# A graph network kernel: the factors of two heads in one mirrored block, and a new order of work

## The chip, the core and the metric

The kernel runs on one core of a Trainium2 chip. The core has five engines, each with its own queue, which it works off in order: TensorE (PE in the profile; its weight loads are shown as PEld) multiplies matrices, VectorE (DVE) and ScalarE (ACT) work element by element, GpSimd (POOL) does small side jobs, and SyncE (SP) issues the transfers between HBM and the on-chip memory SBUF. PE writes to PSUM, from which DVE and ACT read. Engines wait for each other by semaphores. The metric is the device time of one launch in microseconds.

## What is computed

For 16 graphs of 1024 nodes with 256 features: two layers, each with a residual and a layer norm. The first layer weighs the neighbours by a gate, the second is an attention with 4 heads of 64 columns. The change is in the second layer:

```python
Wh = (X @ W).reshape(B, N, H, F)
e_src = jnp.einsum('bnhf,hf->bnh', Wh, a_src)
e_dst = jnp.einsum('bjhf,hf->bjh', Wh, a_dst)
e = jax.nn.leaky_relu(e_src[:, :, None, :] + e_dst[:, None, :, :], LRELU_ALPHA)
mask = (A > 0)[..., None]
e = jnp.where(mask, e, NEG_INF)
alpha = jax.nn.softmax(e, axis=2)
Hout = jnp.einsum('bijh,bjhf->bihf', alpha, Wh)
Hout = jax.nn.elu(Hout)
```

## The kernel before

**The idea of the second layer.** The exponential of a leaky ReLU of a sum is a product of two factors, one of node i and one of node j, with one pair of factors where the sum is positive and another where it is negative. So per head there are two sets of columns of node j: `Wh` times the factor of the positive side (64 columns), `Wh` times that of the negative side (64), and the two factors themselves (2), E = 130 columns in all. A 0/1 matrix `pos` says for which edges the sum is positive. The sum over positive edges is a matmul of `pos` with the 130 columns; the negative side is the sum over all edges less the one over positive edges.

**Precision.** Each factor is held as a high and a low part (l = 0, 1), both in fp32r. They lie in one tile `gm`, by head, block of 128 nodes, part and column.

**Steps** (each is a generator; a step is one `yield`):
- First layer: `aload`, `cast`, `turn`, `mask` bring in and turn the adjacency; `xt`, `xta`, `score` (matmul `e`), `leak`, `leaky`, `sigmoid`, `below`, `lower`, `upper`, `self_loop` make the gate; `agg` multiplies gate and nodes; `residual` adds the bias and makes y; `moments0` (st), `gathered0` (mv), `spread0` (std and rstd, on POOL), `shift0` (DVE) and `norm0` (ACT) are the layer norm of y.
- Second layer: `yt`, `ytc` turn y; `project` is the matmul `pw`; `wh`, `sources`, `rows`, `keep_rows`, `top_dve`, `exps` make the factors, and `product`, `high`, `low` write them into `gm`.
- `pos` (L658): one DVE instruction makes 128 rows (nodes j) by 512 columns (half of the nodes i) for one head. There are 6 buffers.
- `acc` (L670): for each half and head, 8 blocks of j times 4 blocks of i, 32 matmuls of 260 columns: the high and low part of one head (2 x 130), read as one run. Four matmuls use one `pos`.
- `acc_low`, `acc_sum` (L693): ACT copies the low half out of PSUM, DVE adds it to the high half into `u`.
- `all_edges`, `total` (L713): the sums over all edges, without `pos`. Only the second 64 columns and the two factors are needed, 66 of each head: one matmul reads 4 runs of 66 columns for the 4 heads, 264 in all, 16 matmuls (8 blocks, 2 parts) for each block of i.
- `total_kept`, `total_less`, `weigh`, `divide`, `elu`, `join`: difference, weight, division and the elu, on `u`; then the second layer norm and the output.

**What sets the order.** Three tables, `FIRST`, `TIMES` and `LAST` (first graph, the 14 in the middle, last graph), give a place in time for each step of each generator, against the graph's own start; graphs start 112 units apart. `issue` sorts all steps of all graphs by their places and runs them, so that each engine gets its instructions in that order. The places are written out as numbers. No instruction passes another in an engine's queue.

Of the kernel before, what the change touches and what calls it, by code (L numbers as in the profile page):

```python
# [193 lines left out]
def stages(nc, k, pl, b, xg, adjg, outg, sums, span, zinv):  # L194
# [5 lines left out]
    HEADS = [(half, h) for half in range(NH) for h in range(H)]  # L200
# [3 lines left out]
    first, last, late = b == 0, b == k.B - 1, b >= k.B - 2  # L204
# [53 lines left out]
    def aload():  # L258
        for ib in range(NB):
            if first and 2 <= ib < 6:  # L260

                tile = pl.us.tile([P, 2, H, E], F32, tag="us", name="a_us")
                tile = tile.rearrange("p q h e -> p (q h e)")[:, 0:N].bitcast(I32)
            else:
                tile = pl.adjp.tile([P, N], I32, tag="a32", name="a32")
            t["a32", ib] = tile
            nc.sync.dma_start(out=t["a32", ib], in_=adjg[ib * P : (ib + 1) * P, :])
            yield
# [327 lines left out]
    def exps():  # L596
        es = t["es"] = small("es", 2, NB, H)
        nc.scalar.activation(es[:, 1], t["cm"], AF.Exp)
        nc.scalar.activation(es[:, 0], t["cm"], AF.Exp, scale=SLOPE)
        t["rho"] = small("rho", NB, H)  # L600
        nc.scalar.activation(t["rho"], t["sd"], AF.Exp, scale=SLOPE - 1.0)
        yield


    FACTORS = [(h, s) for h in range(H) for s in range(2)]
# [19 lines left out]
    def factor(h, s):  # L625
        if s == 0:
            yield slice(2 * F, E), t["es"][:, :, :, h].rearrange("p s b -> p b s")
        yield slice(s * F, (s + 1) * F), t["prod", h, s]

    def high():  # L630
        for h, s in FACTORS:
            for cols, val in factor(h, s):
                nc.scalar.copy(pl.gm[:, h, :, 0, cols], val)  # L633
            yield

    def low():
        for h, s in FACTORS:
            for cols, val in factor(h, s):
                hi = pl.gm[:, h, :, 0, cols].bitcast(F32)
                nc.vector.tensor_tensor(pl.gm[:, h, :, 1, cols], val, hi, ALU.subtract)  # L640
# [23 lines left out]
    def acc():  # L664
        for half, h in HEADS:
            for pair in range(NQ // 2):
                t["acc", half, h, pair] = pl.ps_u.tile([P, 2, HALF], F32, tag="u", name="acc")
            for jb in range(NB):
                for q in range(NQ):
                    nc.tensor.matmul(  # L670
                        t["acc", half, h, q // 2][:, q % 2, 0 : 2 * E],
                        lhsT=t["pos", half, h, jb][:, q * P : (q + 1) * P],
                        rhs=pl.gm[:, h, jb].rearrange("p l f -> p (l f)"),
# [14 lines left out]
    def acc_sum():  # L688
        for half, h in HEADS:
            for pair in range(NQ // 2):  # L690
                if h == 0:
                    t["u", half, pair] = pl.us.tile([P, 2, H, E], F32, tag="us", name="u")
                nc.vector.tensor_tensor(  # L693
                    t["u", half, pair][:, :, h, :],
                    t["acc", half, h, pair][:, :, 0:E],
                    t["low", half, h, pair], ALU.add,
                )
                yield

# [8 lines left out]
    def total():  # L708
        for ib in TOTALS:
            tot = t["tot", ib] = bank("tot")  # L710
            for jb in range(NB):
                for l in range(2):
                    nc.tensor.matmul(  # L713
                        tot[:, 0 : H * F1],
                        lhsT=t["allm", ib, jb // 4 * 4][:, jb % 4, :],
                        rhs=pl.gm[:, :, jb, l, F:E],
# [5 lines left out]

    def heads_of(tot):
        return tot[:, 0 : H * F1].rearrange("p (h f) -> p h f", h=H)
# [4 lines left out]

    def parts(half, pair, hs):  # L730

        u = t["u", half, pair][:, :, hs]
        return u[..., 0:F], u[..., F : 2 * F], u[..., 2 * F], u[..., 2 * F + 1]

    def second(half, pair):

        return t["u", half, pair][..., F : 2 * F + 1]
# [6 lines left out]
    def total_kept():  # L744
        for ib in TOTALS[:NQ]:
            pair, q = divmod(ib - NQ, 2)
            if q == 0:
                t["ts", pair] = pl.ts.tile([P, 2, H, F1], F32, tag="ts", name="ts")
            nc.scalar.copy(t["ts", pair][:, q], heads_of(t["tot", ib]))
            yield  # L750

    def total_less():
        for ib in TOTALS[NQ:]:
            u = second(0, ib // 2)[:, ib % 2]
            nc.vector.tensor_tensor(u, heads_of(t["tot", ib])[..., 0 : F + 1], u, ALU.subtract)
            yield

    PAIRS = [(half, pair) for half in range(NH) for pair in range(NQ // 2)]  # L760

    def times(val, by):

        if late:
            for q in range(2):
# [8 lines left out]
    def weigh():  # L774
        for half, pair in PAIRS:
            ib, hs = half * NQ + 2 * pair, heads(half)
            u2 = second(half, pair)[:, :, hs]
            if half:
                ts = t["ts", pair][:, :, hs, 0 : F + 1]
                nc.vector.tensor_tensor(u2, ts, u2, ALU.subtract)  # L780
                yield
            times(u2, t["rho"][:, ib : ib + 2, hs])
            yield

    def divide():
        t["rz"] = small("rzs", NB, H)
        for half, pair in PAIRS:
# [4 lines left out]
            rz = t["rz"][:, ib : ib + 2, hs]  # L792
# [8 lines left out]
    def join():  # L801
        for half, pair in PAIRS:
            o, ex, _, _ = parts(half, pair, heads(half))
            yp = nodes(half, pair)[:, :, heads(half)]
            rows = (0, 1) if last and half else (slice(0, 2),)
# [16 lines left out]
    def weigh_end():  # L822
        for h, pair in END:
            if last:
                u2 = second(1, pair)[:, :, h]
                nc.vector.tensor_tensor(u2, t["ts", pair][:, :, h, 0 : F + 1], u2, ALU.subtract)
# [43 lines left out]
    def leave():  # L870
# [32 lines left out]
    "xload": [-190.36],  # L903
    "aload": [-141.21, -134.94, -129.14, -126.41, -107.72, -95.92, -52.91, -49.35],
    "cast": [-133.33, -126.54, -110.85, -106.42, -72.33, -55.28, -40.89, -29.41],
    "turn": [-133.00, -118.97, -108.09, -86.35, -62.89, -45.14, -38.49, -26.07],
    "mask": [-126.25, -118.09, -94.06, -70.56, -52.12, -40.03, -32.69, -25.15],
    "setup": [-54.43, -50.76, -47.38],
    "xt": [-69.63, -66.83, -65.59, -61.38],
    "xtc": [-65.35, -64.69, -63.96, -57.76],  # L910
    "xta": [-60.02, -56.47, -53.23, -47.62, -40.80, -39.84, -35.73, -22.45],
    "score": [
        -55.95, -54.26, -52.86, -52.85, -50.30, -47.61, -41.77, -41.05, -37.61, -36.60,
        -31.53, -19.69,
    ],
    "leak": [
        -54.25, -52.28, -52.05, -51.99, -45.24, -41.19, -38.48, -36.59, -34.23, -28.07,
        -26.47, -19.19,
    ],
    "leaky": [  # L920
        -53.92, -51.61, -45.43, -45.41, -41.52, -40.38, -37.19, -36.20, -32.91, -26.88,
        -25.80, -17.05,
    ],
    "sigmoid": [-50.37, -36.56, -28.45, -23.28, -23.17, -15.81, -5.09, 4.38],
    "below": [-43.48, -40.73, -36.17, -28.75, -25.55, -24.80, -21.22, -11.11, 7.22, 7.95],
    "lower": [-41.97, -37.35, -33.23, -27.18, -24.41, -23.38, -19.01, -9.26, 8.37, 17.62],
    "upper": [-24.74, -21.21, -20.88, -18.06, 1.37, 12.57, 17.16, 22.61],
    "self_loop": [-22.52, -20.95, -18.10, -17.88, 3.26, 14.07, 18.13, 24.49],
    "agg": [
        -18.25, -16.27, -15.06, -15.02, -4.11, -4.03, -2.54, 0.32, 5.09, 8.13, 15.85,  # L930
        17.47, 21.46, 23.59, 23.78, 24.56,
    ],
    "residual": [-8.35, -7.46, -1.27, 2.37, 22.46, 22.48, 26.43, 27.74],
    "moments0": [-5.49, -4.53, 5.61, 8.01, 23.75, 25.11, 27.16, 28.13],
    "gathered0": [4.13, 6.42, 7.91, 10.51, 26.40, 27.32, 28.51, 29.05],
    "spread0": [13.40, 31.26],
    "shift0": [17.29, 31.54],
    "norm0": [21.66, 21.89, 22.47, 23.38, 34.53, 34.91, 35.50, 35.54],
    "yt": [27.46, 27.57, 36.68, 36.99],
    "ytc": [29.00, 29.33, 39.29, 39.57],  # L940
    "project": [32.52, 32.60, 33.90, 39.19, 40.28, 40.33, 40.41, 40.81],
    "wh": [33.22, 36.59, 37.58, 40.10, 40.68, 42.17, 42.34, 43.12],
    "sources": [41.16, 45.78],
    "rows": [41.83, 54.07],
    "keep_rows": [44.82, 56.53],
    "top_dve": [43.38, 45.01, 45.39, 50.81, 51.81],
    "top_pe": [44.42, 46.92],
    "exps": [51.81],
    "product": [53.02, 53.37, 53.98, 54.66, 58.34, 66.43, 69.20, 72.08],
    "high": [53.76, 54.40, 58.33, 58.56, 61.32, 68.49, 71.81, 73.63],  # L950
    "low": [54.19, 57.97, 61.74, 62.89, 71.04, 72.63, 75.29, 76.96],
    "sload": [50.80, 79.07, 83.92, 88.62, 102.34, 116.17, 128.36, 142.07],
    "pos": [
        57.31, 58.08, 60.13, 63.67, 69.85, 70.05, 71.57, 77.68, 80.69, 81.39, 82.09,
        82.79, 83.51, 84.84, 85.08, 85.50, 94.75, 97.25, 97.29, 97.48, 99.31, 100.22,
        100.86, 101.86, 104.39, 105.08, 105.66, 107.42, 108.55, 108.94, 109.06, 109.44,
        111.06, 112.18, 112.18, 112.50, 114.43, 114.99, 117.57, 118.23, 118.61, 122.99,
        125.51, 126.22, 128.00, 128.98, 130.58, 132.32, 133.80, 134.68, 135.40, 135.59,
        136.35, 141.70, 144.45, 144.66, 145.90, 146.60, 148.13, 149.39, 151.16, 153.05,
        156.93, 159.83,  # L960
    ],
    "acc": [
        66.06, 67.27, 68.14, 69.24, 71.32, 72.44, 73.71, 78.80, 83.16, 83.97, 84.72,
        85.39, 85.74, 87.50, 88.94, 90.52, 99.28, 99.52, 100.60, 101.24, 101.47, 101.85,
        102.15, 102.38, 108.43, 108.66, 109.45, 109.46, 109.72, 110.12, 110.70, 110.77,
        114.66, 115.11, 115.34, 116.25, 116.73, 118.20, 118.35, 119.33, 130.24, 130.46,
        130.54, 131.53, 132.09, 132.57, 134.85, 134.91, 141.46, 142.49, 142.93, 144.35,
        145.14, 145.81, 145.91, 146.87, 153.97, 154.83, 159.23, 159.59, 164.73, 165.20,
        165.32, 166.33,
    ],  # L970
    "acc_low": [
        79.49, 79.83, 96.76, 97.23, 103.47, 104.76, 112.24, 112.31, 122.02, 122.21,
        134.93, 135.59, 149.34, 149.98, 169.77, 170.85,
    ],
    "acc_sum": [
        80.66, 80.96, 97.10, 98.04, 105.15, 105.96, 112.53, 112.54, 127.47, 127.48,
# [501 lines left out]
```

## Time and profile before

| | |
|---|---|
| median of 3 runs | 1742.5 us (1742.15 to 1743.12) |
| span of the profiled execution | 1739.6 us |
| PE busy | 1692.1 us (97%) |
| DVE busy | 1639.6 us (94%) |
| ACT busy | 1239.4 us (71%) |
| POOL busy | 106.8 us (6%) |
| `acc` L670: matmuls, mean ns of one | 4096, 292 |
| `tot` L713: matmuls, mean ns of one | 2048, 297 |
| `agg` L427: matmul passes, mean ns of one | 2048, 379 |
| `pos` L658 on DVE: count, mean ns | 1024, 745 |
| u from `acc` and `low` L693 on DVE: count, mean ns | 256, 425 |

A line of the profile names the source line, the engine, the operation, what it writes and reads, the shape, the count, then the busy time in us, the mean duration of one in ns, and the idle time of the engine before it with what ended it. A matmul is pipelined: the next one starts before its duration is over, so its step, from start to start, is less than its duration. An fp32 matmul runs as two passes, and the profile counts passes; an fp32r matmul runs as one. The timeline gives start in us, duration in us and the instruction; equal neighbours are merged.

### The profile page before, as it was taken

What the parts mean: (1) busy time and instruction counts of PE and PEld (TensorE: products, weight loads), DVE (VectorE), ACT (ScalarE), POOL (GpSimd) and SP (SyncE); (2) the same over time, 40 slices, a digit from 0 to 9 for tenths busy, and PEclk for the clock granted to TensorE, in tenths of its full rate; (3) what the DMA queues carried; (4) which work ended last, traced back from release to release, by engine and by line L of the source; (5) the groups of instructions that cost most, each with busy time, mean ns of one, the idle gap of its engine ahead of it and who ended that gap; (6) DMA issues with size and microseconds to landing.
All of it is one profiled execution on the core that took longest, in us unless ns stands there. A gap on an engine that the chain in (4) does not pass through costs nothing.

```text
span 1739.6 us, 29647 instructions
## 1 busy us (share of the span) xinstructions
PE 1692.1 (97%) x10580; PEld 1492.5 (86%) x10580; DVE 1639.6 (94%) x3663; ACT 1239.4 (71%) x2766; POOL 106.8 (6%) x138
## 2 busy tenths in 40 slices
PE   8999999999999999999999999999999999999984
PEld 5789898998979889898998979889898898979883
DVE  5498999999999999999999999999999999999998
ACT  7674957759587685967759587685967859586784
POOL 0000000010000101000010000101000010000100
PEclk9999999999999999999999999999999999999987
DMA  5542333434334343333435334443343424422020
GB/s 190 129 116 67 98 98 92 110 92 131 88 89 101 105 125 92 94 101 92 109 92 129 91 86 102 105 128 91 89 107 92 110 67 117 105 71 55 26 68 26
DMA packets 249005, 168.59 MB, mean 97 GB/s; under 512 B 133010, under 2 KB 232468, under 8 KB 248852
## 3 DMA queue, kind: packets, MB, share of 16 engines
q1 hardware_dynamic: 248848, 166.63, 36.1%
q8 instruction: 86, 1.41, 0.3%
q14 instruction: 67, 0.55, 0.1%
q10 hardware_dynamic: 4, 0.00, 0.0%
HBM read 118.10 MB, written 17.04 MB: 78 GB/s over the span
## 4 chain that ended last, share of the span: by engine, by line
PE 91%; DVE 3%; ACT 2%; DMA 1%; issue 1%; POOL 0%; SPq 0%; ACTq 0%; DVEq 0%; POOLq 0%
PE acc L670 27%; PE agg L427 24%; PE tot L713 14%; PE e L356 13%; PE pw L517 7%; PE pg L395 3%; PE pt L498 2%; PE pt L319 1%; DVE pos L658 1%; DMA sbc<-sdram 1%; ACT prod L614 0%; DMA aT<-a 0%; PE pbc L591 0%; ACT gm L633 0%; ACT y L489 0%
## 5 line engine op out<-in xcount | busy, mean ns | idle before, releaser
L658 DVE SCALAR_TENSOR_TENSOR pos<-sbc,nd,mT 128x512 fp32r<-128x512 f32 x1024 | 737.4, 745 | 10.5 <-PE acc L670 5.0
L670 PE MATMUL acc<-gm,pos 128*128 128x260 f32 x4096 | 608.6, 292 | 8.9 <-DVE gm L640 5.0
L670 PEld LDWEIGHTS acc<-gm,pos 128*128 128x128 f32 x4096 | 536.8, 190 | 19.8 <-issue 5.7
L427 PE MATMUL agg<-xb,gate 128*128 128x256 f32 x2048 | 463.5, 379 | 0.2
L427 PEld LDWEIGHTS agg<-xb,gate 128*128 128x128 f32 x2048 | 379.9, 190 | 47.6 <-DVE gate L419 1.2
L713 PE MATMUL tot<-gm,allm 128*128 128x264 f32 x2048 | 328.8, 297 | 5.4 <-ACT gm L633 4.9
L713 PEld LDWEIGHTS tot<-gm,allm 128*128 128x128 f32 x2048 | 281.4, 189 | 9.7 <-ACT gm L633 5.1
L356 PE MATMUL e<-xT,xTa 128*128 128x512 f32 (+3 forms) x768 | 264.3, 489 | 2.2 <-ACT xTa L344 1.4
L356 PEld LDWEIGHTS e<-xT,xTa 128*128 128x128 f32 x768 | 135.1, 191 | 106.4 <-issue 55.3
L685 ACT COPY low<-acc 128x260 f32<-128x260 f32 x256 | 89.8, 377 | 187.5 <-PE acc L670 187.3
L705 ACT CAST allm<-mT 128x512 fp32r<-128x512 uint8 x256 | 157.4, 615 | 33.4 <-PE tot L713 31.7
L489 ACT ACTIVATE y<-y,shift,rstd 128x256 f32<-128x256 f32 x254 | 136.3, 592 | 48.6 <-DVE shift L477 48.6
L276 ACT ACTIVATE a<-a 128x1024 bf16<-128x1024 int32 x124 | 131.3, 1059 | 32.1 <-DMA aT<-a 23.0
L298 ACT ACTIVATE mT<-aT 128x1024 uint8<-128x1024 bf16 x120 | 127.1, 1059 | 7.6 <-DMA aT<-a 7.5
L468 POOL TENSOR_SCALAR std<-mv 128x4 f32<-128x4 f32 x64 | 27.7, 432 | 1618.7 <-DVE mv L450 1447.1
L517 PE MATMUL pw<-w_aug,yT 128*128 128x264 f32 x512 | 121.8, 387 | 0.5 <-ACT yT L507 0.5
L376 DVE TENSOR_TENSOR gate<-e,gate 128x512 f32<-128x512 f32 x192 | 105.5, 556 | 14.5 <-ACT gate L368 14.4
L693 DVE TENSOR_TENSOR u<-acc,low 128x260 f32<-128x260 f32 x256 | 103.1, 425 | 10.5 <-ACT low L685 10.3
L444 DVE BATCH_NORM_STATS2 st<-y 128x6 f32<-128x256 f32 x256 | 107.5, 421 | 1.2
L517 PEld LDWEIGHTS pw<-w_aug,yT 128*128 128x128 f32 x512 | 93.4, 190 | 15.4 <-ACT yT L507 1.9
L368 ACT ACTIVATE gate<-e 128x512 f32<-128x512 f32 x192 | 90.2, 486 | 13.7 <-PE e L356 13.3
L412 DVE TENSOR_TENSOR gate<-gate,mT 128x1024 f32<-128x1024 f32 (+7 forms) x128 | 96.6, 755 | 2.9 <-ACT mT L298 2.4
(111 smaller groups left out, 1788.8 us busy)
## 6 DMA issues: line engine op xcount, KB each, us to landing
a<-in_adj_dram SPq DMA_DIRECT2D x124, 512.0 KB, 4.6
sbc<-sdram SPq DMA_DIRECT2D x128, 256.0 KB, 4.6
out_dram<-y SPq DMA_DIRECT2D x31, 512.0 KB, 3.5
xb<-in_x_dram SPq DMA_DIRECT2D x15, 1024.0 KB, 5.4
a_us<-in_adj_dram SPq DMA_DIRECT2D x4, 512.0 KB, 8.9
aT<-a SPq DMA_TRANSPOSE x120, 3.1
xb<-in_x_dram SPq DMA_DIRECT2D x2, 512.0 KB, 4.7
sdram<-srow SPq DMA_DIRECT2D x32, 8.0 KB, 1.4
```

Of the source, the lines that this page charges most:

```text
L276: nc.scalar.activation(t["a16", ib], t["a32", ib], AF.Copy, accum_out=sums[:, 0, at : at + 1])
L298: nc.scalar.activation(t["mT"][:, :, ib * P : (ib + 1) * P], t["aT", ib], AF.Square, accum_out=sums[:, 1, at : at + 1],)
L356: nc.tensor.matmul(e[:, 0:n], lhsT=t["xTa", jb][:, c, :], rhs=t["xT"][:, c, at : at + n], start=(c == 0), stop=(c == DC - 1),)
L376: nc.vector.tensor_tensor(ge, t["e", jb, at][:, 0:n], ge, ALU.max)
L427: nc.tensor.matmul(agg[:, 0:D], lhsT=t["gate"][:, jb, ib * P : (ib + 1) * P], rhs=t["xb"][:, jb, :], start=(jb == 0), stop=(jb == NB - 1),)
L444: nc.vector.bn_stats(st, t["y", half][:, q, :])
L489: nc.scalar.activation(y, y, AF.Identity, bias=shift, scale=rstd)
L517: nc.tensor.matmul(pw[:, 0:WD], lhsT=t["yT"][:, c, jb * P : (jb + 1) * P], rhs=k.w_aug[:, c, :], start=(c == 0), stop=(c == DC - 1),)
L658: nc.vector.scalar_tensor_tensor(p_, t["sbc", half, h], t["nd"][:, jb, h : h + 1], t["mT"][:, jb, half * HALF : (half + 1) * HALF], ALU.is ...
L670: nc.tensor.matmul(t["acc", half, h, q // 2][:, q % 2, 0 : 2 * E], lhsT=t["pos", half, h, jb][:, q * P : (q + 1) * P], rhs=pl.gm[:, h, jb] ...
L705: nc.scalar.copy(m_, t["mT"][:, j0 : j0 + 4, ib * P : (ib + 1) * P])
L713: nc.tensor.matmul(tot[:, 0 : H * F1], lhsT=t["allm", ib, jb // 4 * 4][:, jb % 4, :], rhs=pl.gm[:, :, jb, l, F:E], start=(jb == 0 and l == 0),
```

## The change

**The layout.** Two heads share a block of 260 columns for each block of nodes and part. The even head's columns stand as before (positive side 64, negative side 64, factor of the negative side, factor of the positive side), the odd head's mirrored (the two factors, negative side, positive side). The second parts of both, 66 columns each, then lie side by side: 132 columns in one run. So `total` reads two runs of 132 in place of four of 66; `acc` reads one head's columns as two runs of 130 (high and low part), in place of one run of 260. The last graph keeps the old layout.

**What follows from it.** `exps` makes the three factors in a row (slope, one, slope), one Exp more in 15 graphs, so that both kinds of head can copy their pair. `acc_sum` writes a head's 130 columns as two overlapping pieces of 66 (264 elements instead of 260) into `u`, which has 132 columns a head now; the piece of the odd head spoils two columns, which the even head's write puts right. So the heads go in the order 1, 0, 3, 2, in `product`, `high`, `low`, `sload`, `pos`, `acc` and all that follows. Views of `u`, `tot` and `ts` are made anew for `weigh`, `divide`, `join`.

**The tables.** All three tables of places are new. A few lines of each kind are shown.

```diff
+    ORDER = [*range(H)] if last else [h ^ 1 for h in range(H)]
+    HEADS = [(half, h) for half in range(NH) for h in ORDER]
...
-        es = t["es"] = small("es", 2, NB, H)
+        es = t["es"] = small("es", 3, NB, H)
         nc.scalar.activation(es[:, 1], t["cm"], AF.Exp)
-        nc.scalar.activation(es[:, 0], t["cm"], AF.Exp, scale=SLOPE)
+        for s in (0, 2)[: 1 if last else 2]:
+            nc.scalar.activation(es[:, s], t["cm"], AF.Exp, scale=SLOPE)
...
+    AT = [(0, F, 2 * F), (0, F, 2 * F) if last else (F + 2, 2, 0)] * (H // 2)
+
+    def gm_of(h):
+        if last:
+            return pl.gm.rearrange("p (h b l e) -> p h b l e", h=H, l=2, e=E)[:, h]
+        pairs = pl.gm.rearrange("p (g b l i e) -> p g i b l e", g=H // 2, l=2, i=2, e=E)
+        return pairs[:, h // 2, h % 2]
+
+    def gm_second(jb, l):
...
+        pairs = pl.gm.rearrange("p (g b l e) -> p g b l e", g=H // 2, l=2, e=2 * E)
+        return pairs[:, :, jb, l, F : F + 2 * F1]
...
-                        rhs=pl.gm[:, h, jb].rearrange("p l f -> p (l f)"),
+                        rhs=gm_of(h)[:, jb],
...
-                nc.vector.tensor_tensor(
-                    t["u", half, pair][:, :, h, :],
-                    t["acc", half, h, pair][:, :, 0:E],
-                    t["low", half, h, pair], ALU.add,
-                )
+                    at = h // 2 * 2 * (E + 2)
+                    at, step = (at + E + F1, -F1) if h % 2 else (at, F1)
+                    nc.vector.tensor_tensor(
+                        view(t["u", half, pair][:, :], at, [H * (E + 2), 2], [step, 2], [1, F1]),
+                        view(acc[:, :, :], 0, [HALF, 2], [F, 2], [1, F1]),
+                        view(low[:, :, :], 0, [E, 2], [F, 2], [1, F1]), ALU.add,
+                    )
...
-                        tot[:, 0 : H * F1],
+                        by_pair(tot[:, 0 : H * F1]),
...
-                        rhs=pl.gm[:, :, jb, l, F:E],
+                        rhs=gm_second(jb, l),
...
-    "spread0": [13.40, 31.26],
-    "shift0": [17.29, 31.54],
+    "spread0": [19.80, 33.29],
+    "shift0": [20.95, 33.72],
```

**The order that comes out** around the second half of the first layer norm, in a graph of the middle, as the instructions stand in PE's and DVE's queue (`xN`: N in a row; fp32 matmuls counted once, not by passes):

```
before  PE:  agg x12 | pt<-y x8 | acc x16 | pw x4 | acc x8 | pw x2 | acc x8 | pt<-y x8 | pw x10
before  DVE: y | st | mv x2 | pos | y<-u (L810) | u<-u,y (L807) | shift | pos x2 | y<-u | pos | st | pos
after   PE:  acc x12 | pt<-y x4 | agg x8 | pw x6 | acc x28 | pt<-y x4 | acc x4 | pt<-y x4 | pw x4
after   DVE: y | st | mv | pos x2 | shift | pos x2 | u<-u,y (L881) | pos x3 | mv | y<-u (L884) | st | pos
```

PE enters `acc` or `tot` from another kind of matmul 387 times in the order before, 417 times in the new one. ACT loads its function tables 87 times before, 37 times after. All other counts of instructions are the same.

## The prediction

> **What bounds the kernel now.** I read the page's first part, the busy time of the engines over two middle periods, the chain of waits, a stretch of the timeline, and the waits of PE near the end, in this order.
>
> ```profile
> span 1739.6 us, 29647 instructions
> ...
> PE 1692.1 (97%) x10580; PEld 1492.5 (86%) x10580; DVE 1639.6 (94%) x3663; ACT 1239.4 (71%) x2766; POOL 106.8 (6%) x138
> ```
>
> ```profile
> core 0: us, PE busy (x) PEld busy (x) DVE busy (x) ACT busy (x) POOL busy (x), PEclk, DMA share, GB/s
> 847.70:952.20 104.50, 104.50 (x660) 92.70 (x659) 102.34 (x227) 76.05 (x167) 6.60 (x8) 1.00 0.39 102
> 952.20:1056.60 104.40, 104.40 (x658) 92.60 (x658) 102.28 (x227) 75.95 (x166) 6.59 (x8) 1.00 0.38 102
> ```
>
> Each window is one graph's period (from one graph's first `agg` matmul to the next's). PE is busy in all of its 104.4 us, at full clock; DVE in 102.3, so 2.1 us a period are left to it; ACT has 28 idle. So PE sets the period, with no gap left to remove, and DVE stands 2% behind it: any piece of work that DVE delivers late makes a PE gap that nothing gives back. The rest of the span, 1739.6 less 16 periods, is the first graph's start and the end.
>
> The chain of waits gives PE's real step (the mean duration of a matmul overlaps its neighbours):
>
> ```profile
> 888.81 2.87 PE acc L670 x24
> ...
> 894.36 5.18 PE agg L427 x24
> ...
> 907.80 4.45 PE pw L517 x20
> ...
> 937.40 1.50 PE tot L713 x12
> ```
>
> Per matmul: `acc` 119.6 ns for 260 columns in one run, `tot` 125.0 ns for 264 columns in four runs of 66, `agg` 215.8, `pw` 222.5. At `acc`'s rate per column 264 columns would take 121.4, so the four runs cost 3.6 ns more.
>
> **The change on PE: lengths of runs.** It touches 15 of the 16 graphs (the last keeps the old form): 15 x 128 = 1920 `tot` matmuls go from four runs to two, and 15 x 256 = 3840 `acc` matmuls from one run to two. With 3.6 ns spread over three breaks, a break costs 1.2 ns: `tot` gains 1920 x 2.4 = 4.6 us, `acc` loses 3840 x 1.2 = 4.6 us. **Sum 0.** Bounds: `tot` gains all 3.6 and `acc` pays nothing, -6.9 us; `tot` gains half of it (1.8) and `acc` pays 1.8, as an odd head's runs begin at another offset than an even one's, -3.5 + 6.9 = +3.4 us. I take 0, since `acc` in two runs lies between two rows that I have, one run and four.
>
> The Trainium skill ("SBUF — State Buffer", in its note on SBUF cachelines) has lines of 16 bytes and a price for each new line. By it a `tot` of four 264-byte runs touches 68 lines and of two 528-byte runs 66; an `acc` goes from 65 to 66. The row that bears on this is the 3.6 ns. Scaling each row by its lines, an estimate from that page, `tot` would lose 125.0 x 2/68 = 3.7 ns and `acc` gain 119.6/65 = 1.8: -7.1 + 7.1 us, again nothing. The rule speaks against the change, as the cheap side is hit twice as often.
>
> **DVE, ACT, SP.** `acc_sum` adds 264 instead of 260 elements (240 times). From 416 ns for 256 (L459, y) and 691 for 512 (L790, u): 1.07 ns an element, so 4.3 ns x 240 = 1.0 us on DVE, 0.07 a period, hidden in its 2.1 idle; if the interleaved write cost more, 50 ns a call would be 0.8 us a period, which still fits, though it makes every late delivery later. The other operations on `u` keep their counts and sizes (65- and 64-column runs, three free dimensions). ACT gets one Exp of 32 elements in 15 graphs (row L599, 213 ns): 3.2 us, in ACT's idle. In the new order ACT loads its tables 37 times instead of 87: 50 x 1.283 us (row L382) = 64 us of ACT, which wasn't on the path either. SP's queue has the same transfers, at other places. The order of heads 1, 0, 3, 2 costs nothing itself: the two columns that the odd head's sum leaves wrong are written by the even head's, later on the same engine.
>
> **The new order is the term that decides.** Before, in the steady state, the chain holds PE alone; the longest runs of `acc` on PE are 24. In the new order each of 14 graphs has 28 `acc` in a row, at the worst place: last `agg`, 6 `pw`, 28 `acc`. On DVE stand, after that `agg`: y, st, mv, two `pos`, `shift`, two `pos`, one addition to u (L881), three `pos`. `shift` waits for POOL, and behind it are the `pos` that the 28 need (four matmuls use one `pos`). The same sequence, as it runs now:
>
> ```profile
> 1005.45 0.39 DVE L459 TENSOR_TENSOR y<-agg,bias_bc 128x256 f32<-128x256 f32 x1
> 1005.87 0.43 DVE L444 BATCH_NORM_STATS2 st<-y 128x6 f32<-128x256 f32 x1
> ...
> 1006.60 0.63 POOL L468 TENSOR_SCALAR std<-mv 128x4 f32<-128x4 f32 x1 [17.25 <-DVE mv L450]
> ...
> 1007.32 1.33 POOL L469 TENSOR_TENSOR rstd<-std,mhalf 128x4 f32<-128x4 f32 x1
> ...
> 1008.68 0.16 DVE L477 SCALAR_TENSOR_TENSOR shift<-mv,rstd 128x4 f32<-128x4 f32 x1 [0.32 <-POOL rstd L469]
> 1008.76 1.41 DVE L658 SCALAR_TENSOR_TENSOR pos<-sbc,nd,mT 128x512 fp32r<-128x512 f32 x2
> ```
>
> ```profile
> 969.24 2.74 DVE L658 SCALAR_TENSOR_TENSOR pos<-sbc,nd,mT 128x512 fp32r<-128x512 f32 x4
> 971.89 0.43 DVE L459 TENSOR_TENSOR y<-agg,bias_bc 128x256 f32<-128x256 f32 x1
> ```
>
> From y to the `pos` behind `shift` are 3.31 us, whatever DVE does meanwhile, since POOL sets it; a `pos` then takes 0.66 from start to start, 0.75 to its end; the addition to u 0.60 (1002.90 to 1003.50 in this stretch). So, from y's start: the first `pos` begins at 3.31, the second at 3.97, the addition at 4.63, the third `pos` at 5.23, and it ends at 5.98. y itself starts 0.2 us later than PE's next matmul (an `agg` lasts 0.379 by its row and steps by 0.216; 0.04 for the release): 6.18. On PE 6 `pw` (two passes each) take 12 x 0.2225 = 2.67 and 24 `acc` 2.87: the 25th is due at 5.54. The third `pos` behind `shift` is the seventh of this run, the one that the 25th needs. Late by 0.64 us. Now, with `pos` two places ahead of the need and 8 or 16 `acc` at a time between the `pw`, the same wait of `shift` (0.32) reaches no PE gap. What hides it there is that PE has `pw` and transposes between the short runs.
>
> I take 0.6 us x 14 = **+8.4 us**. Bounds: 0, if an older `pos` stands ready, and 0.84 x 14 = +11.8, the whole time that `shift` waits in this order (3.23 less y, st, mv and two `pos`, 0.42 + 0.34 + 0.30 + 1.33 = 2.39). What is late next is the transpose of y's second half and with it the projections, which have only ACT's idle before them, no further loss.
>
> Entering `acc` or `tot` from another kind of matmul happens 417 times in the new order instead of 387. In the chain, four `acc` that follow other work take 0.47 to 0.48 us, where 4 x 0.1196 is 0.478; an entry can't cost over 20 ns. I take +0.2 (0 to 0.6).
>
> The last 160 us have their own table, and there PE does wait (us in total, times, longest):
>
> ```profile
> PE pm L1424 <- DVE bad L1422: 15.3, 1, 15.3
> PE acc L670 <- DVE gm L640: 5.0, 1, 5.0
> PE tot L713 <- ACT gm L633: 4.9, 1, 4.9
> PE acc L670 <- DVE u L693: 3.8, 3, 2.6
> ```
>
> The first is the final check's wait for the output's last steps. Of the other 13.7 us a new order may save or add a few. What can be priced: 44 `acc` of the last graph stand ahead of its first `tot`, where 32 stood, and such a run goes at DVE's pace, 0.66 us for a `pos` against 0.48 for its four `acc`: three more `pos` are +0.5. The last 64 `acc` stand alone in both orders. I take +0.5, bounds -3 and +4. The first graph's start, with some 11 us of PE waits, I leave at 0 (-2 to +2).
>
> **Sum** 0 + 8.4 + 0.2 + 0.5 = +9.1 against the span of 1739.6, so 1748.7. The median of the runs is 2.9 above this execution's span (1742.5); the change doesn't touch what lies around it: **1752**.
>
> **Rivals.** (1) *Faster: the runs of 132 pay and the order holds.* `tot` gains 3.6 ns, `acc` pays nothing, and the late `pos` is there in time, because DVE gets ahead by its 2.1 us a period: 1742.5 - 6.9 + 0.7 = 1736. For it: 130 contiguous columns are long against 66. Against: the chain after `agg` goes through POOL, so spare time on DVE doesn't shorten it. It decides where the gap is under 0.25 us a graph. (2) *No change:* the same gain, the gap as computed: 1742.5 - 6.9 + 8.4 + 0.7 = 1745. (3) *Worse:* `acc` pays as in the upper bound (+3.4), the gap is 0.84 (+11.8), and the end adds 3: 1761. For it: DVE has only 2% left, so that one late transfer or sum pushes several `pos`; against: nothing that DVE does becomes longer by more than 5 ns. That the change doesn't do what it says I leave out: `tot` is built with two runs, and the number of matmuls is the same.
>
> **Numbers.** The forecast has 0.57, its own range 1746 to 1758; rival 1 0.17, rival 2 0.11, rival 3 0.15. 0.2% is 3.5 us, about what can be told from no change: faster (below 1739) 0.17, the same 0.11, slower 0.72. The range goes from 1739, which leaves out most of rival 1, to 1762, above rival 3.
>
> **What would show it.** In the profile after: `tot` at about 122.5 ns a step and `acc` at about 121, in the chain; a gap of 0.6 us on PE in each middle graph, at an `acc` that waits for DVE's `pos` while DVE's `shift` waited about 0.8 for POOL; periods of 105.0 instead of 104.4. If the periods are 104 or less and PE is busy throughout, the step with the late `pos` was wrong. If `acc` stays at 119.6 the price of a break was. If the middle periods are as computed and the time is not, the end was.

## The result, and the profile after

| | before | after |
|---|---|---|
| median (5 runs each) | 1742.5 us (1742.15 to 1744.48) | 1773.35 us (1771.33 to 1776.62) |
| span of the profiled execution | 1739.6 us | 1769.5 us |
| start to the first `agg` | 35.9 us | 35.4 us |
| first period | 76.8 us | 76.8 us |
| the 14 middle periods | 1466.8 us | 1495.8 us |
| from the last graph's first `agg` to the end | 160.2 us | 161.6 us |

The change makes the kernel slower, by a ratio of 1.0174 [1.0163, 1.0185]. The forecast was +9.5 us, the result is +30.9, and 29.0 of the span's 29.9 lie in the 14 middle periods: 2.07 us in each, where 0.6 was forecast.

The page's first part and two groups of its fifth, after:

```profile
span 1769.5 us, 29462 instructions
...
PE 1702.6 (96%) x10580; PEld 1492.8 (84%) x10580; DVE 1647.1 (93%) x3663; ACT 1176.8 (67%) x2731; POOL 110.6 (6%) x138
...
L692 PE MATMUL acc<-gm,pos 128*128 128x260 f32 x4096 | 626.2, 299 | 30.3 <-DVE pos L680 17.5
...
L754 PE MATMUL tot<-gm,allm 128*128 128x264 f32 x2048 | 309.8, 294 | 0.5 <-ACT allm L746 0.5
```

`acc` (L692, before L670) has become longer, 292 to 299 ns, `tot` (L754, before L713) shorter, 297 to 294. Both are small. The new entry is the 30.3 us of idle time ahead of `acc`, most of it waits for `pos`. Two middle periods show the same as a share of the period (columns as before: length, then busy time of each engine):

```profile
859.10:965.60 106.50, 105.20 (x660) 92.70 (x659) 102.19 (x226) 70.61 (x163) 7.07 (x8) 1.00 0.39 100
965.60:1073.30 107.70, 105.76 (x660) 92.57 (x659) 103.53 (x228) 71.42 (x163) 7.07 (x8) 1.00 0.38 99
```

PE was busy in all 104.4 us of a period before; now 1.3 to 1.9 us of each are empty. The clock is 1.00 as before, and ACT has about five us less work per period than before.

**Where the gaps lie.** Counted from PE's starts (a step over 0.08 us longer than the usual one of its form), the gaps of the 14 middle graphs sum to 33.0 us, 4.4 before. By their place after the graph's first `agg`: about 24 us, 13.7 in sum (11 graphs with 0.9 to 1.2 each, and a step 0.1 too long behind it); about 61 us, 11.2 (13 graphs: 0.67, with 0.1 just ahead of it and 0.1 behind it); 16 to 18 us, 1.7. The other 6.4 are 2.0 more than all gaps before; 2.8 of them are 28 steps around `pbc`, 0.1 too long each, which the kernel before has as well. The one at 61 us is the gap of the forecast. The timeline of after there:

```profile
914.57 0.63 POOL L471 TENSOR_SCALAR std<-mv 128x4 f32<-128x4 f32 x1 [18.62 <-DVE mv L453]
...
915.29 1.39 POOL L472 TENSOR_TENSOR rstd<-std,mhalf 128x4 f32<-128x4 f32 x1
...
916.71 0.16 DVE L480 SCALAR_TENSOR_TENSOR shift<-mv,rstd 128x4 f32<-128x4 f32 x1 [0.93 <-POOL rstd L472]
916.79 1.41 DVE L680 SCALAR_TENSOR_TENSOR pos<-sbc,nd,mT 128x512 fp32r<-128x512 f32 x2
...
918.12 0.69 DVE L881 SCALAR_TENSOR_TENSOR u<-u,y 128x512 f32<-128x512 f32 x1
...
918.72 2.07 DVE L680 SCALAR_TENSOR_TENSOR pos<-sbc,nd,mT 128x512 fp32r<-128x512 f32 x3
919.52 0.76 PE L692 MATMUL acc<-gm,pos 128*128 128x260 f32 x4 [0.52 <-DVE pos L680]
```

`shift` waits 0.93 us for POOL, two `pos`, the addition and one more `pos` follow, and PE's `acc` at 919.52 waits for that third `pos`. (The idle time of 0.52 goes by modelled ends; from start to start the step is 0.67 too long.)

The gap at 24 us was in no step of the prediction. The chain of waits of after, which before held PE alone there, shows how it comes about (start, duration, what):

```profile
1293.04 1.05 ACT mT L301 x2
1294.11 3.99 DMA aT<-a
1298.20 1.15 ACT a L279 x2
1299.36 1.28 ACT L890
1300.65 0.64 ACT u L890
1301.29 1.03 ACT mT L301 x2
1302.62 0.77 DVE u L727 x2
1303.39 0.61 DVE u L881
1304.03 0.69 DVE y L884
1304.92 0.66 DVE pos L680
```

It starts in the adjacency of a later graph. `mask` (L301) reads a turned piece; the next transposing DMA (`turn`) may then be issued and takes 3.99 us; `cast` (L279) needs its end, since the bf16 tile that it writes is the one that the DMA reads. Behind `cast` in ACT's queue stand a table load, an exp, the next `mask` and two `acc_low`; DVE's `u` (L727) waits for those, and behind `u` stand the `pos` that PE needs. The timeline of an earlier graph has the amounts, in square brackets:

```profile
763.79 1.06 ACT L279 ACTIVATE a<-a 128x1024 bf16<-128x1024 int32 x1 [4.38 <-DMA aT<-a]
...
768.20 0.77 DVE L727 TENSOR_TENSOR u<-acc,low 128x264 f32<-128x264 f32 x2 [1.97 <-ACT low L709]
...
776.19 0.76 PE L692 MATMUL acc<-gm,pos 128*128 128x260 f32 x4 [1.04 <-DVE pos L680]
```

ACT stands still for 4.38 us, DVE for 1.97 of them, PE for 1.04: each engine swallows a part with the work that it has ahead. The new table has `cast[2]` at -120.51 and `turn[1]`, whose end it needs, at -120.58, 0.07 units ahead. In the old one they stand 8.1 apart (-110.85 and -118.97). The waits of after by pair (us in total, times, longest):

```profile
ACT a L279 <- DMA aT<-a: 63.1, 18, 4.6
...
DVE u L727 <- ACT low L709: 23.4, 15, 2.5
...
DVE shift L480 <- POOL rstd L472: 19.7, 20, 1.5
...
PE acc L692 <- DVE pos L680: 17.5, 25, 1.0
```

The same four before:

```profile
ACT a L276 <- DMA aT<-a: 23.0, 16, 2.8
...
DVE u L693 <- ACT low L685: 10.3, 14, 1.3
...
DVE shift L477 <- POOL rstd L469: 9.0, 17, 1.5
...
PE acc L670 <- DVE pos L658: 0.2, 1, 0.2
```

### The profile page after: what moved, and what is told of

Its sections match the earlier page's. It is cut to its first block, busy times and chain, and to the rows that moved or that the text cites. A ratio compares the mean times of both kernels' runs of the same rounds, so it can differ in the third digit from the quotient of the medians.

```text
span 1769.5 us, 29462 instructions
## 1 busy us (share of the span) xinstructions
PE 1702.6 (96%) x10580; PEld 1492.8 (84%) x10580; DVE 1647.1 (93%) x3663; ACT 1176.8 (67%) x2731; POOL 110.6 (6%) x138
## 5 line engine op out<-in xcount | busy, mean ns | idle before, releaser
L680 DVE SCALAR_TENSOR_TENSOR pos<-sbc,nd,mT 128x512 fp32r<-128x512 f32 x1024 | 723.6, 744 | 1.4 <-PE acc L692 1.0
L692 PE MATMUL acc<-gm,pos 128*128 128x260 f32 x4096 | 626.2, 299 | 30.3 <-DVE pos L680 17.5
L692 PEld LDWEIGHTS acc<-gm,pos 128*128 128x128 f32 x4096 | 541.3, 190 | 68.9 <-DVE pos L680 23.6
L430 PE MATMUL agg<-xb,gate 128*128 128x256 f32 x2048 | 468.6, 380 | 1.2 <-DVE gate L422 1.2
L754 PE MATMUL tot<-gm,allm 128*128 128x264 f32 x2048 | 309.8, 294 | 0.5 <-ACT allm L746 0.5
L754 PEld LDWEIGHTS tot<-gm,allm 128*128 128x128 f32 x2048 | 271.1, 189 | 4.6 <-ACT allm L746 0.8
L709 ACT COPY low<-acc 128x260 f32<-128x260 f32 x256 | 84.4, 372 | 202.4 <-PE acc L692 200.8
L359 PEld LDWEIGHTS e<-xT,xTa 128*128 128x128 f32 x768 | 130.7, 191 | 85.8 <-issue 47.4
L279 ACT ACTIVATE a<-a 128x1024 bf16<-128x1024 int32 x124 | 131.4, 1059 | 66.9 <-DMA aT<-a 63.1
L301 ACT ACTIVATE mT<-aT 128x1024 uint8<-128x1024 bf16 x120 | 126.9, 1058 | 7.1 <-DMA aT<-a 7.1
L520 PE MATMUL pw<-w_aug,yT 128*128 128x264 f32 x512 | 122.1, 388 | 0.4 <-ACT yT L510 0.4
L727 DVE TENSOR_TENSOR u<-acc,low 128x264 f32<-128x264 f32 x240 | 96.1, 426 | 24.4 <-ACT low L709 23.4
L447 DVE BATCH_NORM_STATS2 st<-y 128x6 f32<-128x256 f32 x256 | 103.7, 415 | 1.3
```

The costliest lines, as they stand in the source:

```text
L279: nc.scalar.activation(t["a16", ib], t["a32", ib], AF.Copy, accum_out=sums[:, 0, at : at + 1])
L301: nc.scalar.activation(t["mT"][:, :, ib * P : (ib + 1) * P], t["aT", ib], AF.Square, accum_out=sums[:, 1, at : at + 1],)
L359: nc.tensor.matmul(e[:, 0:n], lhsT=t["xTa", jb][:, c, :], rhs=t["xT"][:, c, at : at + n], start=(c == 0), stop=(c == DC - 1),)
L430: nc.tensor.matmul(agg[:, 0:D], lhsT=t["gate"][:, jb, ib * P : (ib + 1) * P], rhs=t["xb"][:, jb, :], start=(jb == 0), stop=(jb == NB - 1),)
L447: nc.vector.bn_stats(st, t["y", half][:, q, :])
L520: nc.tensor.matmul(pw[:, 0:WD], lhsT=t["yT"][:, c, jb * P : (jb + 1) * P], rhs=k.w_aug[:, c, :], start=(c == 0), stop=(c == DC - 1),)
```

## The experiments

All times are medians in three rounds beside the kernel before on the same chip, 1743.19 us for the first four and 1742.9 for the other four.

**1 and 2: layout and order apart.** The first has the new layout and order of heads with the three old tables of places, the second the old layout with the new ones.

```diff
 TIMES = {
...
-    "cast": [-130.00, -124.39, -120.51, -103.41, -71.16, -47.91, -42.40, -29.83],
-    "turn": [-128.78, -120.58, -113.47, -87.75, -58.61, -46.85, -35.79, -23.68],
+    "cast": [-133.33, -126.54, -110.85, -106.42, -72.33, -55.28, -40.89, -29.41],
+    "turn": [-133.00, -118.97, -108.09, -86.35, -62.89, -45.14, -38.49, -26.07],
...
```

> The changed kernel with the three tables of the kernel before. Theory A (the order costs the time): only the steps of the matmuls differ, 3840 acc at +1.9 ns (119.6 to 121.5 in the two traces) and 1920 tot at -2.6 ns (125.0 to 122.4), so +7.3 - 5.0 = +2.3 us: 1745 us, periods near 104.5 us, no PE gap over 0.2 us in a middle graph. Theory B (the layout makes DVE or PE late, the order only shows it): most of the 31 us stay, 1765 us or more.

> The kernel before with the three new tables; heads in order 0, 1, 2, 3, the old factors. Theory A: the gaps of the new order are there without the layout: 1773 less 2.3 is 1771 us, with PE gaps of about 1.2 us (near 24 us after a graph's first agg) and 0.7 us (near 61 us) in each middle graph. Theory B: 1745 us, no such gaps.

The new layout in the old order takes 1745.85 us, ratio 1.0015 [1.0005, 1.0024]; the old layout in the new order 1772.78, 1.017 [1.0153, 1.0187]. So the order costs the time, and the layout costs 0.15%. In the first neither gap is there, and its middle periods take 2.1 us more than before, about what the lengths of its matmuls make. In the second both gaps are there (1.05 us at 23.6, 0.68 at 60.5), with `tot` and `acc` at their old lengths. Equal pieces of the chain of waits, first before, then the first experiment:

```profile
366.32 2.87 PE acc L670 x24
...
416.90 2.58 PE tot L713 x20
```

```profile
365.81 2.92 PE acc L692 x24
...
416.57 2.53 PE tot L754 x20
```

24 `acc` have become 0.05 us longer, 20 `tot` 0.05 shorter. Over the 15 graphs that have the new layout the mean step of `acc` goes from 119.8 ns to 121.7, that of `tot` from 125.3 to 122.6: 3840 x 1.9 = 7.3 us lost and 1920 x 2.65 = 5.1 gained, +2.2.

**3, 4 and 5: each gap by itself.** The third moves a `cast` and the `mask` of the new table to later places, so that other ACT work comes ahead of the wait; the fifth moves only the second `shift`, behind two more `pos`; the fourth does both.

```diff
-    "cast": [-130.00, -124.39, -120.51, -103.41, -71.16, -47.91, -42.40, -29.83],
+    "cast": [-130.00, -124.39, -117.10, -103.41, -71.16, -47.91, -42.40, -29.83],
-    "mask": [-121.17, -118.70, -101.41, -79.33, -54.12, -37.09, -29.23, -20.61],
+    "mask": [-121.17, -117.00, -101.41, -79.33, -54.12, -37.09, -29.23, -20.61],
```

```diff
-    "shift0": [20.95, 33.72],
+    "shift0": [20.95, 34.58],
```

> The changed kernel; in the table of the middle graphs one step of cast and one of mask, which both wait for the same transposing DMA, are put behind the two copies of low that stood after them in ACT's queue. Theory C (ACT waits 4.4 us for that DMA, and low, the sum into u and the next pos wait behind it): the gap of 1.2 us at 24 us goes, the one of 0.67 us at 61 us stays: 13 graphs x 1.1 = 14 us less, 1759 us. Rival (the late DMA reaches PE anyway, by the mask that needs it): 1770 us or more.

> As the run with cast and mask moved, and the second shift of the first layer norm is put behind the two pos that stood after it in DVE's queue. Theory: both gaps go, 14 x 0.67 = 9 us more than with cast and mask alone: 1750 us; what is left over the kernel before is the steps of the matmuls (+2.3) and some 3 us at the two ends. Rival (the wait for POOL is only moved on to the next pos, as shift now delays y's second half): 1757 us or more.

> The changed kernel with only the second shift of the first layer norm put behind the two pos that stood after it. If the two gaps are independent: the one at 61 us goes, the one at 24 us stays, 14 x 0.67 = 9 us less, 1764 us. If the gaps share a cause, or time won at 61 us is lost again at 24 us: 1770 us or more.

The third takes 1758.7 us (1.0083 [1.0066, 1.01]), the fifth 1762.13 (1.0118 [1.0101, 1.0135]), the fourth 1748.87 (1.0032 [1.002, 1.0045]). The waits of PE's `acc` for `pos`, 25 in after, divide into two kinds. With the `cast` later:

```profile
PE acc L692 <- DVE pos L680: 6.7, 13, 0.5
```

With the `shift` later:

```profile
PE acc L692 <- DVE pos L680: 9.8, 12, 1.0
```

The 13 short ones belong to `shift`, the 12 long ones to `cast`, and each edit leaves the other kind alone. The fifth's timeline at the second `shift`:

```profile
910.25 2.71 DVE L680 SCALAR_TENSOR_TENSOR pos<-sbc,nd,mT 128x512 fp32r<-128x512 f32 x4
912.88 0.15 DVE L480 SCALAR_TENSOR_TENSOR shift<-mv,rstd 128x4 f32<-128x4 f32 x1
```

Four `pos` stand ahead of it where two stood, and no wait is left. Moving `shift` gives 11.2 us between the medians (1773.35 to 1762.13) and 10.8 in the middle periods (1495.8 to 1485.0), which is about the sum of the gaps at 61 us (11.2). Moving `cast` takes 16.4 us off the middle periods (1495.8 to 1479.4), which is about the gaps at 24 and 16 to 18 us (15.4), but puts 3.6 on the first period (80.4 us instead of 76.8; 81.8 in the fourth): graph 1 starts that soon after graph 0, and the new place looks too late for it, which the seventh tries. So the third came out at its expectation of 1759 us by two misses that nearly cancel: more was gained in the middle than the 14 us expected, and the loss in the first period was not foreseen.

**6: what makes the transposing DMA slow.** Twice 512 KB are on their way when the late `turn` is issued: an output and a piece of the adjacency. The sixth moves the output's place behind the `turn` on SP's queue.

```diff
-    "leave": [211.47, 247.00],
+    "leave": [215.60, 247.00],
```

> The changed kernel with the first output transfer (512 KB) put behind the transposing DMA that ACT's cast waits for, in SP's queue, and ACT's order as it is. Theory D (that DMA lands late, 4.45 us after its issue instead of 3.05, since it runs beside two transfers of 512 KB): it lands in about 3.1, ACT's wait falls from 4.4 to some 3.0 us, and of PE's gap at 24 us (1.2) little is left: 1773 - 13 = 1760 us. Rival (the DMA's length has nothing to do with the output, or the other transfer is enough to hold it up): 1770 us or more, landing still over 4 us.

It takes 1767.83 us, 1.0149 [1.0132, 1.0166]: between the two expectations. The timeline of SP's issues in after, then the timeline of the sixth:

```profile
756.43 0.38 SPq L950 DMA_DIRECT2D out_dram<-y  x1
756.86 0.50 SPq L270 DMA_DIRECT2D a<-in_adj_dram  x1
759.23 1.23 SPq L294 DMA_TRANSPOSE aT<-a  x1
```

```profile
751.99 0.36 SPq L270 DMA_DIRECT2D a<-in_adj_dram  x1
...
757.80 1.26 SPq L294 DMA_TRANSPOSE aT<-a  x1
...
759.12 0.56 SPq L950 DMA_DIRECT2D out_dram<-y  x1
...
761.07 1.06 ACT L279 ACTIVATE a<-a 128x1024 bf16<-128x1024 int32 x1 [3.09 <-DMA aT<-a]
...
763.00 0.81 DVE L462 TENSOR_TENSOR y<-agg,bias_bc 128x256 f32<-128x256 f32 x2 [1.17 <-DMA out_dram<-y]
763.48 3.29 PE L430 MATMUL agg<-xb,gate 128*128 128x256 f32 x14 [0.43 <-DVE y L462]
```

With the output behind it the DMA lands 3.12 us after its issue instead of 4.37 (medians at this place), ACT waits 3.09 instead of 4.38, and the gap at 24 us shrinks from 13.7 us in sum to 0.8. So unfinished transfers ahead of the `turn` on SP's queue made it slow. The output by itself isn't shown to be the cause: in after the load of an adjacency piece stands right behind it (756.43 and 756.86), and when the `turn` is issued, the output has 0.4 to 1.9 us left and the load 2.4 to 3.7. With the output out of its way, the load is issued 5.8 us ahead of the `turn` (751.99) instead of 2.4, and has landed by then as well. Other rows speak for the load: with an output alone ahead of it, a `turn` took 3.35 to 3.46 us where the output had 2.0 to 2.2 us left, and 4.37 to 4.78 where it had 3.4 to 3.8 (before and experiments 1 and 8). So what counts there is how long the transfer ahead still takes, and at the late `turn` the load takes longest. No run moves the load alone. But DVE's `y` writes into the buffer that the output is sent from, waits 1.17 us for that transfer, and PE's `agg` waits for `y`: a new gap at 11 to 15 us, 8.6 us in sum. The wait was handed on, from one buffer with no spare to another.

**7: both gaps mended, the first period left alone.** As the fourth, but graph 1 keeps the places of its `cast` and `mask`.

```diff
+        if b == 1:
+            table = dict(
+                TIMES,
+                cast=TIMES["cast"][:2] + [-120.51] + TIMES["cast"][3:],
+                mask=TIMES["mask"][:1] + [-118.70] + TIMES["mask"][2:],
+            )
```

> As the run with cast, mask and shift moved, but in graph 1 cast and mask stay at their old places, as that graph's run there showed 5 us more between the first two graphs' agg (81.8 for 76.8). Theory: 1749 - 5 = 1744 us, the kernel before plus the 2.3 us of the matmuls' steps, less nothing: the same within 0.2%. Rival (those 5 us come from the shift or only move to graph 2): 1749 us.

It takes 1746.28 us, 1.002 [1.001, 1.003]. The first period is 76.8 us again, and PE is busy throughout in these two middle periods:

```profile
741.90:846.50 104.60, 104.60 (x660) 92.40 (x659) 102.66 (x227) 71.16 (x163) 6.58 (x8) 1.00 0.40 102
846.50:951.10 104.60, 104.60 (x660) 92.42 (x659) 101.99 (x226) 70.56 (x163) 6.58 (x8) 1.00 0.41 101
```

Its 14 middle periods take 1469.2 us, those of the first experiment (old order) 1468.9. Three numbers in the table, moved for 13 or 14 graphs, give back nearly all that the new order cost there. It doesn't beat the kernel before: what remains is about what the layout costs alone (1745.85 us in the first experiment).

**8: does the number of runs set a matmul's step, or where they start?** The kernel before with rows of 132 in `gm`, of which 130 are used: `acc` reads two runs of 130 instead of one, `tot` four of 66 as before, but all of them start at a multiple of 16 bytes.

```diff
-                        rhs=pl.gm[:, h, jb].rearrange("p l f -> p (l f)"),
+                        rhs=pl.gm[:, h, jb, :, 0:E],
...
-        pl.gm = pl.big.tile([P, H, NB, 2, k.E], F32R, tag="gm", name="gm")
+        pl.gm = pl.big.tile([P, H, NB, 2, k.E + 2], F32R, tag="gm", name="gm")
```

> The kernel before with gm's rows 132 columns long instead of 130: acc then reads two runs of 130, tot still four runs of 66, but all runs begin at a multiple of 16 bytes. If the number of runs sets the step: acc goes to 121.5 ns (+1.9), tot stays at 125.0: 4096 x 1.9 = +7.8, 1750 us. If where a run begins sets it: tot goes to 122.4 to 123.8, acc stays at 119.8 or a little more: 1738 to 1744 us.

It takes 1752.38 us, 1.0054 [1.0038, 1.0071]. `acc` steps by 122.1 ns, 2.3 more than before, where two runs in after cost 1.8; so a better start saves nothing. `tot` steps by 127.0, 1.8 more than before, which neither theory expected, as it has the same four runs. Why padding makes it dearer wasn't found, and so how much of the 2.3 is the second run and how much the padding stays open too. These are steps between equal neighbours and would make 13 us over the kernel, where 9.5 were measured; over all matmuls of the middle graphs, those that follow another kind included, `acc` takes 2.1 ns more and `tot` 1.2.

## Why the prediction was wrong

| term | forecast, us | measured, us | by |
|---|---|---|---|
| steps of `acc` and `tot` | 0 | +0.9 | mean steps; +2.2 in experiment 1 |
| gap at 61 us (late `pos` behind `shift`) | +8.4 | +11.2 | gaps of after; 10.8 to 11.2 in experiment 5 |
| gap at 24 us, and that at 16 to 18 (late `cast`) | none | +15.4 | gaps of after; 16.4 in experiment 3 |
| other gaps of the middle graphs | none | +2.0 | gaps of after, 6.4, less those before, 4.4 |
| more entries into `acc` and `tot` | +0.2 | not by itself | at most 0.3, below |
| end | +0.5 | +1.4 | span |
| start | 0 | -0.5 | span |

The measured terms sum to 30.4, against 29.9 between the spans; the mean steps differ by up to 0.4 ns between after and experiment 1, so their term is good to about 1 us. The entries are bounded by experiments 7 and 1: without the two gaps the new order costs 0.3 us in the middle periods (1469.2 and 1468.9).

**The step that failed** is the one on "DVE, ACT, SP". It says that "SP's queue has the same transfers, at other places" and takes ACT's idle time as cover, and stops there. A transfer at another place has another neighbour: here `cast` came directly behind the `turn` whose end it needs, and that `turn` directly behind an output and an adjacency piece of 512 KB each. ACT had even become 62.6 us shorter (1239.4 to 1176.8, as forecast: 64 less for table loads, 3 more for the extra Exp), and this was worth nothing, since a queue with idle time still holds all that stands behind one waiting instruction. The prediction walked the new order at one place, where DVE waits for POOL, and not where ACT waits for a DMA. The one-line rival about "one late transfer" was given 1761 without a transfer being looked for.

**The gap of the forecast was right** in its place, its cause and its size: 0.64 worked out, 0.67 measured, at an `acc` that waits for `pos` while `shift` waited 0.93 us for POOL (about 0.8 forecast). The term was mis-sized from 8.4 to 11.2: 13 graphs have it, not 14, but in each a step ahead of it and one behind it lose 0.1 more, 0.86 a graph. That is close to the upper bound of 11.8. Where the 2.0 us of other gaps come from wasn't settled; most of them stand in three graphs.

**The lengths of runs** came out nearly as named: over the 15 graphs with the new layout `tot` steps by 122.3 ns and `acc` by 121.6, with 122.5 and 121 forecast. The means before are 125.3 and 119.8, so 1920 x 3.0 = 5.8 us are gained and 3840 x 1.75 = 6.7 lost, +0.9 for a forecast of 0: a break in `acc` costs 1.75, where the two taken out of `tot` gave 3.0 together. An odd head's other offset, which the bound feared, does nothing: the odd heads step by 121.7 and 121.3, the even ones by 121.3 and 122.0. The 16-byte lines of the Trainium skill ("SBUF — State Buffer", note on SBUF cachelines), of which the prediction made an estimate of -3.7 and +1.8 ns, come close to these -3.0 and +1.75. In experiment 8 the same count of lines would make an `acc` 66 lines instead of 65, +1.8 ns (2.3 measured), and leave `tot` at 68 lines, where 1.8 more were measured: there the page doesn't explain the row.

**The rest.** DVE's addition to `u` takes 426 ns on average, 425 before; it was priced at 4 ns more and is hidden either way. The end costs 1.4 us, forecast 0.5 for a run of 44 `acc`; but experiment 1, which has the old order there, loses 1.6 at the end as well, with the last wait of PE at 16.4 us instead of 15.3. So the reason given isn't the one, and the real one was not followed up. PE filled the whole period again wherever the gaps were gone (experiments 1, 7 and 8).

## What to carry to other kernels

When an order of work is made anew, look for every instruction that waits for a transfer or another engine and ask, on its own queue, what now stands right behind it: a cast put 0.07 units behind the DMA that frees its buffer cost some 15 us, and three numbers in a table took them and the other gap away. Change a layout and an order in separate steps; here the one costs 0.15% and the other 1.7%, and together they look like one bad idea. Before a matmul's runs are traded, count how often each side of the trade is executed: twice as many `acc` lose 1.75 ns as `tot` gain 3.0. And see in what order a queue issues its transfers: here a load stood behind an output, and the `turn` that mattered behind both.

## What the runs showed of the hardware

A transposing DMA of one piece lands 3.05 us after its issue (median) when no transfer issued ahead of it is still on its way, and in 3.12 with others issued 1.3 us behind it (experiment 6). With an output and an adjacency piece of 512 KB each ahead of it, at the place of the late `cast`, it took 4.0 to 4.7. Another in the chain of waits had a piece of 256 KB (`sbc`) and one of 1 MB (`xb`) ahead, the last of which landed 5.4 us after this one's issue, and it landed 0.9 later:

```profile
1484.25 6.32 DMA aT<-a
```

The Trainium skill ("DMA: Bandwidth & Descriptors", Rules for kernel authors) says that transfers from different issuers run on the same 16 engines and interleave; all of these come from one issuer, SP, so no run here shows that.

An fp32r matmul of 260 columns pays 1.75 ns (1.9 in experiment 1) when its operand comes in two runs of 520 bytes instead of one of 1040, and 2.3 in experiment 8, where both runs start at multiples of 16 bytes but the padding made `tot` 1.8 ns dearer too.
